# A two-layer kernel with a learned-weight 7x7 convolution: the position term of four of twelve slots is given as the bias of ScalarE's reads

## The chip, the cores and the metric

The kernel runs on one core of a Trainium2 chip. The metric is the device time of one execution in microseconds. Before the change the median of three runs is 3290.9 us (3275.71 to 3295.12). Everything is computed in float32.

## The reference, cut to what matters

The input has 4 images of 256 channels and 56 x 56 pixels. Layer 0 is the convolution in which the change lies; layer 1 is an attention with a squared score and a feed-forward part on selected tokens, and the change does not touch it.

```python
x1 = conv1x1(x, w1, b1)                       # 32 channels
x2 = conv1x1(x, w2, b2)                       # 32 channels
x3 = conv1x1(x, w3, b3)                       # 256 channels
p = conv1x1(position(h, w), wp, bp)           # 2 channels, the same for all images
sub2 = x1[:, :, None] - unfold_patches(x2)    # 49 shifts, reflected border
subp = p[:, :, None] - unfold_patches(p)
feat = concatenate([sub2, subp], axis=1)      # 34 channels, 49 shifts, 3136 pixels
y = relu(bn_eval(feat, bn1))
y = conv1x1(y, cw1)                           # 34 -> 32
y = relu(bn_eval(y, bn2))
wgt = softmax(conv1x1(y, cw2, cb2), axis=2)   # over the 49 shifts
out = sum over the 49 shifts of shifted(x3) * wgt, each weight shared by 8 channels
```

The "position term" is what the two channels of `subp`, after their normalisation and relu, add to the first hidden layer (`cw1`). `position` is linear along rows and along columns, so `p` minus shifted `p` is one constant for all pixels whose shifted pixel lies inside the image, and differs only where the border is reflected.

## The kernel before, in words

**Tiling.** The convolution works on blocks of 4 image rows: 14 blocks an image, 56 in all (`blocks`, line 417). A block has 4 x 56 = 224 pixels (`FB4`). The 48 shifts other than the centre are packed as 12 slots of 4 shifts each (`SLOTS`, line 79): a tile has 128 partitions, which are 4 shifts times 32 channels, and a slot is 224 columns of it. `PARTS` (line 86) splits the slots into part 0 (slots 0 to 7) and part 1 (slots 8 to 11, "the last four"). All of part 1 has the way `ROW`. The centre shift ("own") goes by its own small path.

**Steps of a block.** `relation` (line 521): `differ` subtracts on GpSimd into `y1`; `bend` is the relu of that on ScalarE, with nothing else; `hidden(i)` (line 558) makes the hidden layer of one part on TensorE into the PSUM tile `quad`, which has 4 banks, indexed by `r`, the row group of the matmuls; `bend_more(i)` (line 578) reads all four banks with relu, scale `s2` and bias `t2` into `y2`. `softmax` (line 600): `logits`, the maxima on VectorE, and later `lowered`, `exponents` and the sum. `values` (line 729): ScalarE copies a slot's weight to a PSUM bank (`weights`), VectorE multiplies it with the shifted values (`product`; GpSimd does slots 2, 5, 8 and 11), and TensorE adds the product into `acc` (`add`). `divide` makes `o`, and the result is stored.

**The hidden layer.** `hidden(i)` runs 16 matmuls of 32 x 32 (4 row groups by 4 column groups) and then 4 position matmuls, one for each row group, of 32 rows by 128 columns. With `m` = 2 for part 0 and 1 for part 1, these stream 448 or 224 columns of the constant tile `places` and accumulate into `quad`. `kind` (line 524) is 0 for the first block of an image, 2 for the last, 1 for the 12 between; it chooses the rows of weights in `cw1p`, so that one constant tile serves the three cases. `places` is made once, in `positions` (line 279), in the opening before the blocks.

**Order of the work.** Engines run in program order (`InOrder`, line 999; every instruction of the convolution so has line 1007 in the profile). The order is fixed by a table: each step of block k is entered at `k * ROUND + AT[name]`, with `ROUND` = 249 (line 109) and `AT` from line 110, and the entries are sorted. Near the change it is: `bend_1` 36, `bend_0` 51, `hidden_1` 52, `bend_more_1` 53, `values_1` 67, `hidden_0` 77, `bend_more_0` 90, `logits_0` 99, `largest_0` 126, `logits_1` 141. The adds and copies of the block before lie between these. There is one `quad`: `hidden_1`, `hidden_0`, `logits_0`, `logits_1`, `lowered_0` and `lowered_1` follow one another in it, and each waits until its last reader is done.

**Two kinds of round.** `planes` (line 295) prepares the normalised input in chunks of 8 image rows, one chunk in every second round until the input is used up. Such a round has more TensorE matmuls (`small<-xb` in the profile), two of them (`values_0` and `values_1`) on either side of `hidden_1`. The other rounds have `both` and `keep_both` of the same chunk, or no step of it at the end.

**Queues.** Nearly all transfers are issued by the SyncE queue; GpSimd issues indirect ones in layer 1.

Of the kernel before, what the change touches and what calls it, by code (L numbers as in the profile page):

```python
# [7 lines left out]
F32 = mybir.dt.float32  # L8
I32 = mybir.dt.int32
AF = mybir.ActivationFunctionType  # L10
ALU = mybir.AluOpType
# [4 lines left out]
P = 128  # L16
# [5 lines left out]
PAD = 3  # L22
# [31 lines left out]
def view(t, offset, dims):  # L54

    return bass.AP(t.tensor, t.offset + offset, [list(t.ap[0])] + [list(d) for d in dims])
# [29 lines left out]
PARTS = ((0, 8), (8, 12))  # L86
# [4 lines left out]
RB = 4  # L91
# [6 lines left out]
FB4 = RB * W  # L98
# [35 lines left out]
def conv_layer(  # L134
# [5 lines left out]
    const = ctx.enter_context(tc.tile_pool(name="conv_const", bufs=1))  # L140
# [5 lines left out]
    ve, te, se, sy, gp = (  # L146
        InOrder(tc, e) for e in (nc.vector, nc.tensor, nc.scalar, nc.sync, nc.gpsimd)
    )
# [3 lines left out]
    group = lambda g: slice(g * REL, (g + 1) * REL)  # L152
# [8 lines left out]
    def constant(name, of, shape):  # L161
        t = const.tile(shape, F32, name=name)
        nc.scalar.dma_start(t, of)
        return t
# [19 lines left out]
    cw1p = constant("cw1p", d["cw1_pos_tile"], [P, 3, P])  # L184
# [10 lines left out]
    quad = banks.tile([P, 4, 512], F32, name="quad")  # L195
# [10 lines left out]
    def bank():  # L206
        free.append(free.pop(0))
        return free[-1]
# [37 lines left out]

    tbc = const.tile([P, 1], F32, name="tbc")
    places = const.tile([P, 3 * FB4], F32, name="places")
    pp = opening.enter_context(tc.tile_pool(name="pos", bufs=1, side="right"))
    loc = pp.tile([P, 2, 2, 3 * FB4], F32, name="loc")  # L250
    nc.scalar.dma_start(loc, d["loc"])
# [27 lines left out]
    def positions():  # L279

        pl = pp.tile([P, 2, 3 * FB4], F32, name="pl")
        ve.tensor_scalar(pl, loc[:, 0], pposs[:, 4:5], None, ALU.mult)
        ve.scalar_tensor_tensor(pl, loc[:, 1], pposs[:, 5:6], pl, ALU.mult, ALU.add)
        ve.tensor_scalar(pl, pl, pposs[:, 6:7], None, ALU.add)
        ve.tensor_tensor(places, pl[:, 0], pl[:, 1], ALU.subtract)
        yield
        se.activation(places, places, AF.Relu, bias=tp1, scale=sp1)
        yield
        own = pp.tile([8, 1], F32, name="ownpos")
        se.activation(own, tp8, AF.Relu)  # L290
        p = bank()
        te.matmul(p[:, :1], cw1pd, own, start=True, stop=True)
        ve.tensor_scalar(tbc, p[:, :1], s2, t2, ALU.mult, ALU.add)
# [119 lines left out]
    y2 = [yp.tile([P, 4, (e - a) // 4, FB4], F32, name=f"y2_{a}") for a, e in PARTS]  # L413
# [107 lines left out]
    def relation(k):  # L521

        n, b = blocks[k]
        kind = 0 if b == 0 else 2 if b == last_block else 1

        def differ(i):
            aw, a1, _ = held["a", k]
            t = 3 * i
            ki, kj, way = SLOTS[t]
            if way == ROW:  # L530
                first, step = aw[:, ki : ki + RB, kj : kj + W], 1
            else:
                r = (4 * (COL_QUADS * n + b) + ki) % AC_KEPT
                first, step = ac[:, r : r + RB, kj : kj + W], WP
            gp.tensor_tensor(
                y1[:, t : t + 3].rearrange("p t (h w) -> p t h w", w=W),
                a1[:, :, PAD : PAD + W].unsqueeze(1).to_broadcast([P, 3, RB, W]),
                bass.AP(
                    first.tensor, first.offset,
                    [list(first.ap[0]), [step, 3], [WP, RB], [1, W]],  # L540
                ),
                ALU.subtract,
            )

        def differ_own():
            aw, _, aq = held["a", k]
            c = held["c1", k] = smp.tile([P, W], F32, tag="c1", name=f"c1_{k}")
            gp.tensor_tensor(c, aq, aw[:, PAD, PAD : PAD + W], ALU.subtract)

        def bend(i):  # L550
            a, e = PARTS[i]
            se.activation(y1[:, a:e], y1[:, a:e], AF.Relu)

        def bend_own():
            c = held["c1", k]
            se.activation(c, c, AF.Relu)

        def hidden(i):
            a, e = PARTS[i]
            m = (e - a) // 4  # L560
            for r in range(4):
                for j in range(4):
                    te.matmul(
                        quad[group(j), r, : m * FB4], cw1[group(r)],
                        view(y1[group(r)], (a + j) * FB4, [[4 * FB4, m], [1, FB4]]),
                        start=True, stop=False, skip_group_check=True,
                    )
            for r in range(4):
                te.matmul(
                    quad[:, r, : m * FB4], cw1p[group(r), kind],  # L570
                    places[group(r), a // 4 * FB4 : (a // 4 + m) * FB4],
                    start=False, stop=True, skip_group_check=True,
                )

        def hidden_own():
            quartered(small[:, :W], cw1d, held["c1", k], start=True, stop=True)

        def bend_more(i):
            m = (PARTS[i][1] - PARTS[i][0]) // 4
            se.activation(  # L580
                y2[i].rearrange("p r m f -> p r (m f)"), quad[:, :, : m * FB4], AF.Relu,
                bias=t2, scale=s2,
            )

        def bend_more_own():
            c = held["c2", k] = smp.tile([P, W], F32, tag="c2", name=f"c2_{k}")
            se.activation(c, small[:, :W], AF.Relu, bias=tbc, scale=s2)

        for i in range(4):
            yield f"differ_{i}", differ, (i,)  # L590
        yield "differ_own", differ_own, ()
        yield "bend_own", bend_own, ()
        yield "hidden_own", hidden_own, ()
        yield "bend_more_own", bend_more_own, ()
        for i in range(2):
            yield f"bend_{i}", bend, (i,)
            yield f"hidden_{i}", hidden, (i,)
            yield f"bend_more_{i}", bend_more, (i,)
# [281 lines left out]
    opening_steps = [{name: (do, of) for name, do, of in planes(0, q)} for q in range(3)]  # L880
    made_values = ("values_0", "keep_values_0", "values_1", "keep_values_1", "edges_values")
    placed = positions()
    for q in range(2):
        go(q, "normal_0", "normal_1", "both")
# [960 lines left out]
def tile_hybrid(tc: tile.TileContext, d, out: bass.AP):  # L1845
    with tc.tile_pool(name="scratch", bufs=1, space=DRAM) as dram:
        xs = dram.tile([NB, C, HW], F32, name="xs")
        us = [dram.tile([HW, ROW_N], F32, name=f"us{b}") for b in range(NB)]
        ln0 = dram.tile([C, HW], F32, name="ln0")
        rs0, rs0n = (dram.tile([1, HW], F32, name=f"rs0{i}") for i in "ab")  # L1850
        with tc.tile_pool(name="early", bufs=1) as pool:
            early = [
                pool.tile([P, *shape], F32, name=f"early{i}")
                for i, shape in enumerate(((2, 3 * C), (2, CH), (CH,)))
            ]
            conv_layer(tc, d, xs, ln0, rs0, rs0n, early)
            attn_ffn_layers(tc, d, xs, ln0, rs0n, us, out, early)
# [157 lines left out]
```

## Time and profile before

| | |
|---|---|
| median of three runs | 3290.9 us |
| lowest and highest run | 3275.71 and 3295.12 us |
| the profiled execution's own time | 3285.6 us |
| its span, first to last instruction | 3283.8 us |
| granted TensorE clock, mean over the span | 0.981 |
| position matmuls of 448 columns (part 0) | 448 instructions, 57.9 us busy |
| position matmuls of 224 columns (part 1) | 448 instructions, 38.8 us busy |
| ScalarE's read of `quad` for part 0, 128 x 1792 | 56 instructions, mean 1846 ns |
| ScalarE's read of `quad` for part 1, 128 x 896 | 56 instructions, mean 1091 ns |

How to read the lines of the profile: a group line gives the engine, the operation, the tile written and the tiles read (`quad<-places,cw1p`), the shape, the number of instructions, then the busy time in us and the mean of one in ns, and then how long the engine stood idle just before these and what ended it. A timeline line gives the start in us from the span's start, the length in us of a run of like instructions, and in square brackets the idle time before it with what released it. PE is TensorE's matmul, PEld its weight load, DVE VectorE, ACT ScalarE, POOL GpSimd, SP SyncE. A float32 matmul appears as two MATMUL instructions, so 4 position matmuls are 8 lines of the trace. Ends of matmuls are modelled, so a group's length reaches a little past the start of the next group.

### The profile page before, as it was taken

Reading aid. Unit: us, or ns where it says so; the run is one execution under the profiler, and the core shown is the slowest. Engines: PE = TensorE matmul, PEld = TensorE weight load, DVE = VectorE, ACT = ScalarE, POOL = GpSimd, SP = SyncE. Lnnn points to the kernel's source line nnn. Section 1 sums busy time; section 2 is a strip of 40 time slices with the busy share of each in tenths; the row PEclk is TensorE's granted clock in tenths of the full one; section 3 lists DMA queues with packets and bytes.
Section 4 is the critical chain, followed back from the end, with each engine's and each line's share of the span. In section 5 each row is a group of like instructions: output and inputs, shape, how many; then the busy total and the mean of one; then the engine's idle time right before and its main releaser. Section 6 shows DMA issues by size and latency. Waiting matters only on the chain. (4 is left out here: it accounts for less than half of the span.)

```text
span 3283.8 us, 108590 instructions
## 1 busy us (share of the span) xinstructions
PE 3040.2 (93%) x47392; PEld 1331.7 (41%) x47392; DVE 2230.9 (68%) x3022; ACT 1564.4 (48%) x2923; POOL 1722.4 (52%) x1223
## 2 busy tenths in 40 slices
PE   5999999999999999979999899989999899989899
PEld 2333333333333333324333443334333343356566
DVE  4888888998888888867455766567655765443121
ACT  4556566666566565523455244533455235531111
POOL 2899898999899899956101430236022430202311
PEclk8999999999999999989999999999999899999999
DMA  7656676567566655440122002310123001321110
GB/s 225 170 151 174 158 191 179 152 179 193 152 162 170 173 154 147 115 119 2 28 67 64 27 10 61 98 40 19 39 76 84 16 6 46 102 67 53 51 46 23
DMA packets 276930, 327.56 MB, mean 100 GB/s; under 512 B 96033, under 2 KB 270277, under 8 KB 276325
## 3 DMA queue, kind: packets, MB, share of 16 engines
q1 hardware_dynamic: 266469, 298.84, 34.5%
q0 software_dynamic: 7824, 19.48, 1.8%
q8 instruction: 372, 6.09, 0.8%
q10 hardware_dynamic: 2160, 2.29, 0.2%
q14 instruction: 105, 0.86, 0.1%
HBM read 251.51 MB, written 68.51 MB: 97 GB/s over the span
## 5 line engine op out<-in xcount | busy, mean ns | idle before, releaser
L1007 ACT ACTIVATE ph<-pg,unit 128x896 f32<-128x896 f32 x448 | 427.2, 1004 | 413.7 <-PE pg L1007 413.1
L1007 PE MATMUL acc<-pr,same 128*32 128x448 f32 x5376 | 595.8, 544 | 15.3 <-POOL pr L1007 8.3
L1007 POOL TENSOR_TENSOR phi<-ls 128x512 f32<-128x512 f32 (+1 forms) x200 | 247.0, 1235 | 494.8 <-issue 229.0
L1007 POOL TENSOR_TENSOR pr<-xw,w 128x1792 f32<-128x1792 f32 (+2 forms) x126 | 413.6, 3307 | 102.9 <-ACT exp L1007 80.0
L1007 DVE TENSOR_TENSOR pr<-xc,exp 128x1792 f32<-128x1792 f32 (+2 forms) x247 | 441.5, 1840 | 30.8 <-ACT exp L1007 27.5
L1007 DVE TENSOR_TENSOR pr<-xw,exp 128x1792 f32<-128x1792 f32 (+1 forms) x252 | 447.6, 1804 | 1.2 <-ACT exp L1007 1.2
L1007 POOL TENSOR_TENSOR pr<-xc,w 128x1792 f32<-128x1792 f32 (+1 forms) x135 | 419.6, 3117 | 9.6 <-ACT w L1007 6.6
L1007 POOL DMA_INDIRECT us<-rows,to x112 | 112.9, 1008 | 592.5 <-DVE rows L1007 329.3
L1007 DVE TENSOR_TENSOR phi<-pv,ls 128x1408 f32<-128x1408 f32 (+1 forms) x200 | 321.6, 1618 | 55.0 <-PE accs L1007 46.5
L1007 PE MATMUL quad<-y,cw 32*32 32x224 f32 (+1 forms) x10752 | 299.5, 456 | 30.6 <-ACT w L1007 18.8
L1007 PE MATMUL pg<-qT,pairs 32*128 32x448 f32 x1792 | 273.6, 587 | 6.2 <-ACT ph L1007 3.8
L1007 PE MATMUL pv<-early,xn 128*32 128x256 f32 x3136 | 220.9, 396 | 52.7 <-DVE phi L1007 34.1
L1007 ACT ACTIVATE ls<-pv 128x256 f32<-128x256 f32 (+1 forms) x200 | 77.4, 387 | 397.0 <-PE pv L1007 384.3
L1007 PE MATMUL accs<-phi,v 128*32 128x512 f32 (+1 forms) x1600 | 221.4, 617 | 32.0 <-DVE phi L1007 31.0
L1007 PEld LDWEIGHTS acc<-pr,same 128*32 128x32 f32 x5376 | 132.5, 109 | 240.2 <-issue 140.7
L1007 PE MATMUL acc<-ph,cf 128*32 128x448 f32 (+1 forms) x1792 | 215.5, 553 | 0.0
L1007 ACT ACTIVATE h<-ph,apar 128x512 f32<-128x512 f32 (+1 forms) x104 | 63.3, 659 | 295.6 <-PE ph L1007 295.6
L1007 DVE TENSOR_REDUCE mm<-quad 128x56 f32<-128x1792 f32 x112 | 172.7, 1542 | 32.2 <-PE quad L1007 32.1
L1007 ACT ACTIVATE y<-quad,bn2t,bn2s 128x896 f32<-128x896 f32 x112 | 164.5, 1468 | 63.0 <-PE quad L1007 63.0
L1007 POOL TENSOR_TENSOR y<-a,ac 128x672 f32<-128x672 f32 x112 | 171.0, 1526 | 36.3 <-DMA ac<-a12d 36.3
L1007 ACT ACTIVATE w<-quad,par 128x1792 f32<-128x1792 f32 x112 | 154.3, 1377 | 66.7 <-PE quad L1007 65.9
L1007 PEld LDWEIGHTS quad<-y,cw 32*32 32x32 f32 x10752 | 85.4, 103 | 244.0 <-issue 118.4
(282 smaller groups left out, 4960.2 us busy)
## 6 DMA issues: line engine op xcount, KB each, us to landing
xw<-x3d SPq DMA_DIRECT2D x54, 992.0 KB
xc<-x3d SPq DMA_DIRECT2D x58, 248.0 KB
xc<-x3d SPq DMA_DIRECT2D x58, 247.5 KB
xc<-x3d SPq DMA_DIRECT2D x58, 247.0 KB
xc<-x3d SPq DMA_DIRECT2D x58, 246.5 KB
x3d<-sx SPq DMA_DIRECT2D x28, 496.0 KB
xr<-in_x_own SPq DMA_DIRECT2D x56, 224.0 KB
xs<-xr SPq DMA_DIRECT2D x224, 56.0 KB
```

Source lines behind the costliest of these rows:

```text
L1007: return lambda *a, **k: self.tc.keep_in_program_order(of(*a, **k))
```

## The change

For part 1 the constant of the inner pixels is taken out of `places` and put into the bias of the second-layer read.

In the opening, `inner` takes one inner column of the last slot group of `places`, and that slot group has this column subtracted, so that its inner columns become zero. Twelve matmuls with one column each (4 row groups, 3 kinds) multiply `inner` by the position weights, and one VectorE instruction turns them into `lifts`, the bias of each kind and row group (times `s2`, plus `t2`).

In `hidden(1)`, in blocks of kind 1, the 4 position matmuls stream only the 3 left and 3 right columns of the 4 image rows, 24 columns in place of 224, in the pattern `[[W, 4], [W - PAD, 2], [1, PAD]]`. In blocks of kind 0 and 2 they keep 224 columns. Part 0 keeps its 448.

`bend_more(1)`, in all blocks, becomes four activations, one for each bank of `quad`, each with its own bias from `lifts`, 224 columns each, in place of one of 4 x 224. The step keeps its place in the order, and so does every other one.

```diff
@@ -246,6 +246,9 @@
     places = const.tile([P, 3 * FB4], F32, name="places")
+    LIFTED = PARTS[1][0] // 4
+    inner = const.tile([P, 1], F32, name="inner")
+    lifts = const.tile([P, 3, 4, 1], F32, name="lifts")
@@ -286,6 +289,20 @@
         se.activation(places, places, AF.Relu, bias=tp1, scale=sp1)
         yield
+        mine = places[:, LIFTED * FB4 : (LIFTED + 1) * FB4]
+        ve.tensor_copy(inner, mine[:, W // 2 : W // 2 + 1])
+        ve.tensor_tensor(mine, mine, inner.to_broadcast([P, FB4]), ALU.subtract)
+        yield
+        for r in range(4):
+            for kind in range(3):
+                te.matmul(
+                    quad[:, r, kind : kind + 1], cw1p[group(r), kind],
+                    inner[group(r)], start=True, stop=True,
+                )
+        ve.tensor_scalar(
+            lifts, view(quad, 0, [[1, 3], [512, 4], [1, 1]]), s2, t2, ALU.mult, ALU.add
+        )
+        yield
         own = pp.tile([8, 1], F32, name="ownpos")
@@ -565,10 +582,11 @@
+            of = [[W, m * RB], [W - PAD, 2], [1, PAD]] if i and kind == 1 else [[1, m * FB4]]
             for r in range(4):
                 te.matmul(
-                    quad[:, r, : m * FB4], cw1p[group(r), kind],
-                    places[group(r), a // 4 * FB4 : (a // 4 + m) * FB4],
+                    view(quad[:, r], 0, of), cw1p[group(r), kind],
+                    view(places[group(r)], a // 4 * FB4, of),
                     start=False, stop=True, skip_group_check=True,
                 )
@@ -577,6 +595,12 @@
         def bend_more(i):
             m = (PARTS[i][1] - PARTS[i][0]) // 4
+            for r in range(4 * i):
+                se.activation(
+                    y2[i][:, r, 0], quad[:, r, :FB4], AF.Relu, bias=lifts[:, kind, r], scale=s2
+                )
+            if i:
+                return
             se.activation(
                 y2[i].rearrange("p r m f -> p r (m f)"), quad[:, :, : m * FB4], AF.Relu,
                 bias=t2, scale=s2,
```

## The prediction, made before the changed kernel had run

> **What bounds the kernel now.** First the totals of the page, then the convolution alone (stretch table, 90 to 1430 us; columns are PE, PEld, DVE, ACT, POOL busy, granted clock, DMA share), since the change lies there only.
>
> ```profile
> PE 3040.2 (93%) x47392; PEld 1331.7 (41%) x47392; DVE 2230.9 (68%) x3022; ACT 1564.4 (48%) x2923; POOL 1722.4 (52%) x1223
> ```
>
> ```profile
> 90.00:1430.00 1340.00, 1283.83 (x26032) 495.75 (x26024) 1179.54 (x937) 811.78 (x1528) 1222.39 (x638) 1.00 0.61 161
> ```
>
> TensorE 96%, GpSimd 91%, VectorE 88%, ScalarE 61%: three engines near full, at full clock. None is "the" bound; the order of the hand-overs decides. So I read the timeline round by round. A round is one block of four image rows. Rounds 2, 4, ... 48 also prepare a chunk (matmuls `small<-xb`): 24 long rounds, about 24.4 us from one divide `o` to the next; 31 others are short, about 22.7 us; block 0 stands by itself. Short round, TensorE and then ScalarE:
>
> ```profile
> 814.47 0.67 PE L1007 MATMUL quad<-y,cw 32*32 32x224 f32 x32 [0.31 <-ACT w L1007]
> 815.08 0.66 PE L1007 MATMUL quad<-places,cw1p 32*128 32x224 f32 x8
> 815.67 0.96 PE L1007 MATMUL acc<-pr,same 128*32 128x448 f32 x8
> 816.80 0.96 PE L1007 MATMUL acc<-pr,same 128*32 128x448 f32 x8 [0.17 <-DVE pr L1007]
> 817.69 1.05 PE L1007 MATMUL quad<-y,cw 32*32 32x448 f32 x32
> 818.67 0.66 PE L1007 MATMUL quad<-places,cw1p 32*128 32x448 f32 x4
> ```
>
> ```profile
> 815.82 0.35 ACT L1007 ACTIVATE exp<-w 128x224 f32<-128x224 f32 x1
> 816.10 1.09 ACT L1007 ACTIVATE y<-quad,bn2t,bn2s 128x896 f32<-128x896 f32 x1
> 817.08 0.36 ACT L1007 ACTIVATE exp<-w 128x224 f32<-128x224 f32 x1
> 817.36 0.54 ACT L1007 ACTIVATE sa<-small,sh,bn1s 128x224 f32<-128x224 f32 x1
> 817.78 0.25 ACT L1007 ACTIVATE wo<-wo 128x56 f32<-128x56 f32 x1
> ```
>
> The fourth TensorE line is the one to see: the second add starts 1.13 us after the first, where adds one behind the other take 0.75 to 0.78, because VectorE's product ends at 816.7. What TensorE gains ahead of 816.8 is lost there. Long round:
>
> ```profile
> 838.17 0.68 PE L1007 MATMUL quad<-places,cw1p 32*128 32x224 f32 x8
> 838.77 1.77 PE L1007 MATMUL small<-xb,w 128*128 128x448 f32 x4
> 840.48 1.71 PE L1007 MATMUL acc<-pr,same 128*32 128x448 f32 x16
> 842.12 1.05 PE L1007 MATMUL quad<-y,cw 32*32 32x448 f32 x32
> 843.10 1.03 PE L1007 MATMUL quad<-places,cw1p 32*128 32x448 f32 x8
> ```
>
> Here nothing waits: TensorE is back to back. What it gains passes on to the add before GpSimd's third product (its buffer comes free there):
>
> ```profile
> 822.03 7.36 POOL L1007 TENSOR_TENSOR pr<-xw,w 128x1792 f32<-128x1792 f32 x2 [0.33 <-DMA ac<-a12d]
> ```
>
> ```profile
> 846.46 3.68 POOL L1007 TENSOR_TENSOR pr<-xw,w 128x1792 f32<-128x1792 f32 x1 [2.25 <-ACT exp L1007]
> ```
>
> In both kinds of round it starts 0.20 us after the modelled end of that add (821.83 and 846.26), whatever releaser the view names. TensorE, then two GpSimd products, then TensorE from 829.44 or 853.85: that is the chain, and time gained or lost by `hidden_0` is on it.
>
> **The change, part by part.**
>
> Position matmuls of the last four slots, 48 of the 56 blocks: 224 columns become 24. From group start to the next group 448 columns take 0.97 us and 224 take 0.59 (815.08 to 815.67), so 0.0017 us a column and, for 24, 0.25 us. The eight weight loads of this group alone span 0.31. Saved: 0.28 to 0.34, I take 0.30. No row shows a write in runs of three columns, so the other end is 0; the nearest row, `acc<-po` with 112 columns in two runs, takes 259 ns against 260 for a whole run (`small<-lsq`), so I stay at 0.30. The Trainium skill (PSUM — Partial Sum Buffer, Specifications (TRN2)) says that any non-contiguous pattern slows matmuls significantly. By the row the sum below stands; by that rule, taken as the saving lost, it would be 6.3 us higher, and no row here shows that.
>
> Second read of the hidden layer, all 56 blocks: one read of 896 becomes four of 224. The old one takes 1.09. The nearest row has the same shape, source and both pointers: `sa<-small`, 0.537 mean, and its follower starts 0.42 after it (817.36, 817.78). Four: 3 x 0.425 + 0.537 = 1.81, so +0.72 a block; bounds 1.68 (the `xr<-xr` pair's interval of 0.39) and 2.15 (no overlap). By the Trainium skill (ScalarE: Activation LUTs, What ACT_TABLE_LOAD costs) an activation costs 186 ns, 93 for each pointer, 0.833 per element, less 93 back to back: an estimate of +0.84, which would add 0.12 to each late round, some 4 us. ScalarE has 39% idle, so only two things matter.
>
> (a) Behind the reads on ScalarE stands the copy `exp<-w`, for which VectorE's next product waits. Short round: it lands at 817.44, becomes 818.16, and is needed at 818.65: free. Long round: it lands at 841.34, becomes 842.06, and is needed at 842.07: just free; what is late there has 0.83 us more cover, VectorE's later wait for `quad` at 847.65. ScalarE waits 0.46 and 0.70 us for others before its next read of `quad` and so catches up.
>
> (b) `hidden_0` overwrites `quad`. Behind it on TensorE's queue are its position term, the sums, the add that frees GpSimd's buffer, and the logits; ScalarE, GpSimd and VectorE wait for those. Each read now touches one bank, so I take it that each quarter of `hidden_0` waits for its own bank: free at 0.54, 0.96, 1.39 and 1.81 after the start. Short rounds: 816.10 + 1.81 + 0.05 (the hand-over from a `quad` reader at 825.25 to matmuls at 825.30) = 817.96; the last quarter starts now 0.12 behind the first, 817.81. Late by 0.15; in most short rounds `hidden_0` comes 0.07 earlier, so 0.22. I take 0.20; bounds 0.05 (reads of 1.68) and 0.34 (whole tile held). TensorE's 0.30 is not set against this: the product at 816.7 eats it, and the reads start behind ScalarE's own relu and copy, not behind TensorE. Long rounds: reads start 1.83 after the position term, last bank free at 3.69; the last quarter needs it at 3.95 - 0.30 + 0.12 = 3.77. Free, and all of the 0.30 passes. The three long edge rounds (no saving) lose nothing.
>
> Opening: a column copy, a subtraction, 24 one-column matmul passes, one small VectorE operation, once. They fall in TensorE's wait of 1.16 us before `small<-ownpos` (38.0 us) and VectorE's 12.5: nothing; about 1 us uncovered. Block 0's `hidden_0` has 0.27 us of room and gets 0.54 less: 0.4 with the smaller of these. No DMA is added, and none moves on SP's or GpSimd's queue.
>
> Sum: long interior rounds 21 x -0.30 = -6.3; short rounds 31 x +0.20 = +6.2; opening +0.4; together +0.3. The profiled execution took 3285.6 (span 3283.8 and 1.8 around it), 5.3 under the median shown, so 3285.9 here and 3291 beside that median.
>
> **The rivals.**
>
> *Whole-tile release.* `hidden_0` starts only when the fourth read ends: 31 x 0.34 = 10.5, long rounds gain 0.26 (3.95 to 3.69): -5.5. With 0.4: +5, 3296. For it: before, one read holds all four banks, so the trace cannot tell.
>
> *Reads wholly hidden.* Short rounds lose nothing and the DVE wait moves along with TensorE: 48 x 0.33 = -16, 3275. Against it: the add at 816.80.
>
> *No shorter matmul.* Runs of three cost as much as 224 columns: 0 - 0 + 6.2 + 0.4, 3298.
>
> *ScalarE becomes the bound (slower).* Place: the copy after the reads. If it reaches VectorE late in every round by the whole addition: 56 x 0.72 = +40, 3331. It decides once the copy is more than 0.5 us late in short rounds, that is, once the four reads take over 2.3 us. Against it: even without overlap they take 2.15. For it: long rounds have 0.01 us left before VectorE waits.
>
> **How the numbers follow.** Chances: forecast 0.45, whole-tile 0.24, hidden 0.14, no shorter 0.09, ScalarE bound 0.08. About 1% (33 us) is what a measurement of this kernel can tell from no change. Only the ScalarE case passes it upward: slower 0.08. Nothing worked out here passes it downward; 0.03 is left for a chain that I have misjudged. Within: 0.89. The low end is the hidden case less 5 us of the runs' own spread, 3270. The high end adds up the bad bounds: 31 x 0.34, no saving, and the copy exposed in the 24 long rounds (17.3): +28, 3319. Outside lie the ScalarE case and tails.
>
> **What would show it.** Right: a `quad<-places` group of 24 columns of about 0.3 us; four reads of about 0.54, 0.42 apart; short rounds about 0.2 longer, interior long rounds 0.3 shorter; the add at 816.80 still waiting for VectorE. Wrong: VectorE waiting for `exp` in short rounds; `hidden_0` starting at the last read (whole-tile); GpSimd's third product no later in short rounds.

## The result and the profile after

The changed kernel takes 3296.43 us (median of 20 runs, 3288.43 to 3318.36) against 3286.37 for the kernel before in the same comparison (20 runs, 3275.71 to 3295.12). The ratio is 1.0036 with a 95% interval of 1.0023 to 1.0049: about 12 us slower (7.6 to 16), where the forecast was +0.3. That is still inside the 1% that the forecast called no change and inside its range, but the interval, of 0.13% to either side, excludes zero, so a term of the sum was off. The forecast came out right because its range also held the case of a rival, and that rival is what happened: the case it chose, a release bank by bank, did not. The profiled execution of the changed kernel has a time of 3294.97 and a span of 3293.2 us.

First the totals and the stretch of the convolution from the profile after (columns as before: PE, PEld, DVE, ACT, POOL busy, granted clock, DMA share).

```profile
PE 3026.9 (92%) x47416; PEld 1331.3 (40%) x47416; DVE 2237.6 (68%) x3025; ACT 1602.3 (49%) x3091; POOL 1721.9 (52%) x1223
```

```profile
90.00:1430.00 1340.00, 1263.32 (x25882) 492.71 (x25872) 1170.42 (x926) 844.49 (x1679) 1205.88 (x634) 1.00 0.62 161
```

TensorE has 13 us less work in all, ScalarE 38 us more, and the time grew: no total of busy time tells the outcome. In the fixed stretch GpSimd fell from 1222 to 1206 us because the stretch now holds less of the work (634 of its instructions instead of 638). The cause has to be read in the rounds. The same short round as in the prediction, TensorE and then ScalarE, after the change:

```profile
823.71 0.42 PE L1031 MATMUL quad<-places,cw1p 32*128 32x24 f32 x8
824.06 0.96 PE L1031 MATMUL acc<-pr,same 128*32 128x448 f32 x8
825.43 0.96 PE L1031 MATMUL acc<-pr,same 128*32 128x448 f32 x8 [0.41 <-DVE pr L1031]
826.69 1.05 PE L1031 MATMUL quad<-y,cw 32*32 32x448 f32 x32 [0.30 <-ACT y L1031]
827.66 1.03 PE L1031 MATMUL quad<-places,cw1p 32*128 32x448 f32 x8
```

```profile
824.45 0.35 ACT L1031 ACTIVATE exp<-w 128x224 f32<-128x224 f32 x1
824.73 1.81 ACT L1031 ACTIVATE y<-quad,lifts,bn2s 128x224 f32<-128x224 f32 x4
826.42 0.37 ACT L1031 ACTIVATE exp<-w 128x224 f32<-128x224 f32 x1
```

Three things are to be seen. The position group, 823.71 to the next group at 824.06, is 0.35 us instead of 0.59. The second add now waits 0.41 for VectorE where it waited 0.17: what TensorE gained is lost there, as forecast. And the fourth line has a wait that was not there: `hidden_0` (`quad<-y`, 448 columns) waits 0.30 for ScalarE. The four reads end at 824.73 + 1.81 = 826.54, and `hidden_0` starts at 826.69, 0.15 behind the end of the last of them (0.144 before rounding). It was not released bank by bank. Measured from the start of the position group it starts at 2.98 us instead of 2.54 (the medians; 2.61 in the round shown before). GpSimd's third product follows:

```profile
831.02 7.35 POOL L1031 TENSOR_TENSOR pr<-xw,w 128x1792 f32<-128x1792 f32 x2 [0.69 <-ACT exp L1031]
```

It starts 7.31 us after the position group, which is also the median of the short rounds; before, the median was 6.88. The lateness of `hidden_0`, 0.44, arrives there almost whole (0.43).

The long round behind it, TensorE and ScalarE:

```profile
847.16 0.43 PE L1031 MATMUL quad<-places,cw1p 32*128 32x24 f32 x8
847.52 1.77 PE L1031 MATMUL small<-xb,w 128*128 128x448 f32 x4
849.23 1.71 PE L1031 MATMUL acc<-pr,same 128*32 128x448 f32 x16
850.95 1.05 PE L1031 MATMUL quad<-y,cw 32*32 32x448 f32 x32
```

```profile
848.99 1.81 ACT L1031 ACTIVATE y<-quad,lifts,bn2s 128x224 f32<-128x224 f32 x4
```

`hidden_0` starts at 850.95, that is at 3.79 instead of 3.95. The reads end at 850.80, 0.15 ahead of it again: TensorE could have come 0.25 earlier and is held for the last 0.09, although the view shows no wait there.

The median starts of `hidden_0`, in us after the position group of part 1, over all rounds of one profile, and the median change of a round's length. A round's length is taken from one position group of part 1 to the next and compared with the same round of the profile before; of the long rounds, the 21 interior ones count:

| kernel | short rounds | long rounds | round's length, short / long | time against before |
|---|---|---|---|---|
| before | 2.54 | 3.95 | |  |
| after | 2.98 | 3.79 | +0.45 / -0.14 | +11.8 us |
| `e1_narrow_only` | 2.54 | 3.70 | +0.01 / -0.26 | 0.0 |
| `e9_narrow_no_opening` | 2.54 | 3.71 | +0.02 / -0.24 | -8.5 |
| `e2_four_reads_only` | 2.97 | 3.95 | +0.41 / +0.01 | +14.5 |
| `e10_four_reads_long_rounds` | 2.54 | 3.95 | 0.00 / +0.03 | -0.3 |
| `e6_read_behind_copy` | 3.15 | 3.95 | +0.61 / +0.02 | +12.5 |
| `e7_eight_reads_only` | 3.95 | 4.76 | +1.40 / +0.81 | +66 |

The last column is the ratio less one, times 3286 or so; the intervals stand with each experiment. A ratio is worked out from all timed runs of a comparison, so it can differ a little from the quotient of the two medians. Single profiles differ by several us through rounds that wait for transfers, so the last column is from the timed rounds and not from spans.

### The profile page after: what moved, and what is told of

Its sections match the earlier page's. It is cut to its first block, busy times and chain, and to the rows that moved or that the text cites. A ratio compares the mean times of both kernels' runs of the same rounds, so it can differ in the third digit from the quotient of the medians.

```text
span 3293.2 us, 108812 instructions
## 1 busy us (share of the span) xinstructions
PE 3026.9 (92%) x47416; PEld 1331.3 (40%) x47416; DVE 2237.6 (68%) x3025; ACT 1602.3 (49%) x3091; POOL 1721.9 (52%) x1223
## 5 line engine op out<-in xcount | busy, mean ns | idle before, releaser
L1031 ACT ACTIVATE exp<-w 128x224 f32<-128x224 f32 x448 | 156.9, 355 | 45.2 <-DVE pr L1031 43.5
```

The source lines that it names most:

```text
L1031: return lambda *a, **k: self.tc.keep_in_program_order(of(*a, **k))
```

## The experiments

Three theories were set against one another. **Release**: the loss comes from `hidden_0`, which waits for the end of the last read, in the short rounds, and the gain comes from the long interior rounds alone. **Whole saving**: the shorter matmuls gain in all 48 interior blocks, some 12 us, and the reads cost still more, some 22. **Load**: the added ScalarE time itself is what costs, by making ScalarE's copies late for VectorE.

### The matmuls alone, and the reads alone

`e1_narrow_only` is the changed kernel with the one read and one bias of before:

```diff
-            for r in range(4 * i):
-                se.activation(
-                    y2[i][:, r, 0], quad[:, r, :FB4], AF.Relu, bias=lifts[:, kind, r], scale=s2
-                )
-            if i:
-                return
```

> The changed kernel with one read of the second part, with bias t2, in place of four: the matmuls of 24 columns alone. It leaves the constant of the inner pixels out of the result. The changed kernel is about 10 us over the one before. Theory Release (TensorE's gain counts only in the long rounds; the loss is hidden_0 waiting for the last of the four reads in short rounds): the position group takes 0.35 in place of 0.60, hidden_0 comes 0.25 earlier in the 21 long interior rounds and not at all in short ones, so about -5 us, ratio 0.998 to 0.999. Theory Whole saving (the gain counts in all 48 interior blocks and the reads cost some 22 us): 48 x 0.25 = -12 us, ratio 0.996. Theory Load (the loss is ScalarE's added time, which makes its copies late for VectorE): the gain is as in one of the two, no loss.

Measured: 3285.87 against 3283.69, ratio 1.0000 (0.9983 to 1.0016). A saving of 12 us is outside this interval, unless the opening's work gives it back (see `e8_opening_only`). The 5 us that Release expected from the long rounds lie just inside it: they are neither seen nor excluded, although `hidden_0` does start at 3.70 there.

`e2_four_reads_only` is the kernel before with four reads, all with the bias `t2`:

```diff
+            for r in range(4 * i):
+                se.activation(
+                    y2[i][:, r, 0], quad[:, r, :FB4], AF.Relu, bias=t2, scale=s2
+                )
+            if i:
+                return
```

> The kernel before with four reads of one bank each, all with bias t2; the position matmuls keep 224 columns; the result is the same. Theory Release: short rounds lose 0.43 (hidden_0 from 2.54 to 2.98 us after the position term), long ones nothing (the last read ends at 3.64, hidden_0 stands at 3.95): 31 x 0.43 + 0.5 = +14 us, ratio 1.004. Theory Whole saving: +22 us, ratio 1.007. Theory Load: 56 x 0.72 at the most, between +14 and +40 us, with VectorE waiting for copies longer than before in long rounds also.

Measured: 3300.79 against 3283.69, ratio 1.0044 (1.0027 to 1.0062), +14.5 us. The four reads alone cost all of the loss and a little more.

`e3_two_reads_only` reads two banks at a time:

```diff
+            for r in range(0, 4 * i, 2):
+                se.activation(
+                    y2[i][:, r : r + 2, 0], quad[:, r : r + 2, :FB4], AF.Relu, bias=t2, scale=s2
+                )
+            if i:
+                return
```

> The kernel before with two reads of two banks each, bias t2, the result the same: ScalarE's time per block grows by about 0.22 in place of 0.72. Theory Release: the last read ends at 1.02 + 1.31 = 2.33 after the position term, with 0.15 of hand-over at 2.48, before the 2.54 at which hidden_0 stands in most short rounds: 0 to +2 us, ratio 1.000 to 1.0006. Theories Whole saving and Load: a share of 0.22 / 0.72 of what four reads cost, +4 to +7 us, ratio 1.0013 to 1.002.

Measured: 3288.71 against 3283.69, ratio 1.0006 (0.9990 to 1.0022). No cost can be told from zero. In the short round the two reads end just early enough for `hidden_0`:

```profile
823.97 1.33 ACT L1013 ACTIVATE y<-quad,bn2t,bn2s 128x448 f32<-128x448 f32 x2
```

The position group of this round is at 822.95 in its profile, so the reads end at 2.35; `hidden_0` keeps its median of 2.54. ScalarE's added time is a third of that of four reads (0.24 against 0.72), so this run alone does not part Release from Load.

### The change only where it should pay

`e4_long_rounds_only` narrows the matmuls and splits the reads in the 21 long interior rounds alone; the others have the kernel's old form. `places` stays whole, and a small tile `border` holds the subtracted border columns.

```diff
+        lifted = kind == 1 and k % 2 == 0 and k <= 48
...
+            of = [[W, m * RB], [W - PAD, 2], [1, PAD]] if i and lifted else [[1, m * FB4]]
...
+                    border[group(r)] if i and lifted
+                    else view(places[group(r)], a // 4 * FB4, of),
...
+            for r in range(4 * i * lifted):
```

> The change made only in the 21 interior blocks whose round is long; the other 35 keep the whole constant tile and one read. The result is the same as before. Theory Release: hidden_0 stands at 3.79 in place of 3.95 us in these rounds and where it was in short ones: 21 x -0.16 = -3 us, ratio 0.999, perhaps not to be told from 1. Theory Load (late copies cost as much as four reads, in proportion to the rounds): 21 / 56 of ScalarE's part of the loss less the gain of 21 x 0.25, 0 to +3 us.

Measured: 3283.44 against 3285.92, ratio 0.9994 (0.9977 to 1.0012). No loss and no gain can be told from zero; the typical long interior round is 0.14 shorter, which would make 21 x 0.14 = 3 us. This is the version that the readings point to, and it is not shown to beat the kernel before.

### ScalarE's time without a hold, and a hold without ScalarE's time

`e5_scalar_load` adds three small activations behind the read of before. They write tiles that nothing reads and touch no part of `quad`:

```diff
+            for t in spare if i else ():
+                se.activation(t, places[:, :8], AF.Relu, bias=t2, scale=s2)
```

> The kernel before with its one read, and behind it three ScalarE instructions of 8 columns each into tiles that nobody reads: about 0.73 us more on ScalarE at the same place, as the four reads add, but quad is released when it was before. The result is the same. Theory Release: 0 to +2 us, ratio 1.000 to 1.0006, and hidden_0 at 2.54 and 3.95 us as before. Theory Load: the same loss as four reads alone, +14 us or more, ratio 1.004 or more, with VectorE waiting for copies.

Measured: 3289.26 against 3283.69, ratio 1.0021 (1.0007 to 1.0034), +7 us (2 to 11). That is more than Release expected, and the Load theory has a part in it. The three take 0.95 us, more than the 0.72 that the change adds. Where they hurt is to be read in round 29 of that profile, VectorE and then ScalarE:

```profile
769.58 4.00 DVE L1010 TENSOR_TENSOR pr<-xc,exp 128x1792 f32<-128x1792 f32 x2
774.17 2.02 DVE L1010 TENSOR_TENSOR pr<-xc,exp 128x1792 f32<-128x1792 f32 x1 [0.59 <-ACT exp L1010]
```

```profile
772.95 0.95 ACT L1010 ACTIVATE spare<-places,bn2t,bn2s 128x8 f32<-128x8 f32 x3
773.79 0.34 ACT L1010 ACTIVATE exp<-w 128x224 f32<-128x224 f32 x1
...
774.86 1.03 ACT L1010 ACTIVATE lsq<-lt 128x448 f32<-128x448 f32 x2
```

The same three products run without a gap in the kernel before:

```profile
766.49 5.93 DVE L1007 TENSOR_TENSOR pr<-xc,exp 128x1792 f32<-128x1792 f32 x3
```

Here VectorE waits 0.59 for a copy (`exp`) that ScalarE makes only after the added work. The two squares for the next layer's norm (`lsq`) belong to the same round but come behind that copy, so they do not delay it. What differs is how early VectorE wants it: in the kernel before, the copy of round 29 was ready 0.20 us before VectorE's next product started, and in the round that the prediction read, 1.15. The wait occurs in short rounds 1, 9, 13, 19, 29, 33, 39 and 45, with 0.36 to 1.30 us each and 5.9 together, and in none of them in the kernel before (waits over 0.15 us count); that is most of the 7 us.

`e6_read_behind_copy` is the opposite test. The read stays one, with no work added, but is entered behind a copy of the block before, so that it ends later:

```diff
-    "keep_values_0": 47, "bend_0": 51, "hidden_1": 52, "bend_more_1": 53, "values_1": 67,
+    "keep_values_0": 47, "bend_0": 51, "hidden_1": 52, "bend_more_1": 71, "values_1": 67,
```

> The kernel before with its one read of the second part moved behind the next copy of a weight (its place in the order 71 in place of 53); nothing is added to ScalarE, and that copy comes earlier for VectorE. The result is the same. Theory Release: in short rounds the copy waits until VectorE frees its bank, 1.64 us after the position term; the read then runs from 1.9 to 3.0, hidden_0 at 3.1 in place of 2.54: 31 x 0.59 = +18 us, ratio 1.0055; long rounds are as before. Theory Load: 0 or a little less, ratio 0.999 to 1.000.

Measured: 3298.89 against 3285.92, ratio 1.0038 (1.0019 to 1.0058), +12.5 us. A late release alone, with ScalarE's work as before, costs as much as the whole change. The short round shows it, ScalarE and TensorE:

```profile
832.31 1.08 ACT L1007 ACTIVATE y<-quad,bn2t,bn2s 128x896 f32<-128x896 f32 x1
```

```profile
831.98 0.96 PE L1007 MATMUL acc<-pr,same 128*32 128x448 f32 x8 [0.17 <-DVE pr L1007]
833.54 1.20 PE L1007 MATMUL quad<-y,cw 32*32 32x448 f32 x32 [0.60 <-ACT y L1007]
```

The read ends at 833.39 and `hidden_0` starts 0.15 later. Over the 30 short rounds that have a next round, without the latest one, `hidden_0` starts 0.49 later on average than before (2.95 against 2.46): 31 x 0.49 = 15, of which 12.5 was measured (6 to 19 by the interval).

`e7_eight_reads_only` doubles the suspected hold: eight reads of half a bank, bias `t2`.

```diff
+            for r in range(4 * i):
+                for f in (slice(0, FB4 // 2), slice(FB4 // 2, FB4)):
+                    se.activation(
+                        y2[i][:, r, 0, f], quad[:, r, f], AF.Relu, bias=t2, scale=s2
+                    )
+            if i:
+                return
```

> The kernel before with eight reads of half a bank each, bias t2, the result the same; ScalarE gets some 1.65 us more a block. Theory Release: the reads last 7 x 0.33 + 0.43 = 2.74; short rounds: hidden_0 at 1.02 + 2.74 + 0.15 = 3.91 in place of 2.54, 31 x 1.37 = +42; long rounds: 4.72 in place of 3.95, 24 x 0.77 = +18; together +61 us, ratio 1.0185. Theory Load, in proportion to what ScalarE's time alone cost (7 us for 0.73): +16 us, ratio 1.005; in proportion to four reads (14.5 us for 0.72): +33 us, ratio 1.010.

Measured: 3354.56 against 3285.92, ratio 1.0200 (1.0173 to 1.0226), +66 us. Release, with the hold now in the long rounds as well, had 1.0185. The short round:

```profile
857.18 2.79 ACT L1014 ACTIVATE y<-quad,bn2t,bn2s 128x112 f32<-128x112 f32 x8
```

```profile
857.88 0.96 PE L1014 MATMUL acc<-pr,same 128*32 128x448 f32 x8 [0.17 <-DVE pr L1014]
860.12 1.21 PE L1014 MATMUL quad<-y,cw 32*32 32x448 f32 x32 [1.27 <-ACT y L1014]
```

The reads end at 859.97, and once more `hidden_0` starts 0.15 behind the last. In the long rounds, where four reads were free, it now waits 0.74 and starts at 4.76. VectorE also waits for the copy behind the reads here, in 29 of the 30 short rounds that have a next round, so not all of the 66 us has to be the hold.

### The opening, and the matmuls without it

`e8_opening_only` adds the opening's work to the kernel before, with the subtraction into a tile that nothing reads:

```diff
+        ve.tensor_copy(inner, mine[:, W // 2 : W // 2 + 1])
+        ve.tensor_tensor(pl0, mine, inner.to_broadcast([P, FB4]), ALU.subtract)
...
+                te.matmul(
+                    quad[:, r, kind : kind + 1], cw1p[group(r), kind],
+                    inner[group(r)], start=True, stop=True,
+                )
```

> The kernel before with the opening of the change alone: the column, the subtraction (into a tile that nobody reads), the 24 one-column passes and the bias are made and not used. The result is the same. Both theories: 0 to +1 us, ratio 1.000. If it is +4 us or more, part of the loss is the opening's.

Measured: 3291.02 against 3285.92, ratio 1.0014 (0.9995 to 1.0032): not to be told from zero. The prediction gave the new instructions nothing, or about 1 us if nothing covers them.

`e9_narrow_no_opening` has the 24-column pattern of `hidden(1)` alone:

```diff
+            of = [[W, m * RB], [W - PAD, 2], [1, PAD]] if i and kind == 1 else [[1, m * FB4]]
```

> The kernel before with the 24-column position matmuls alone: no opening work, the constant tile is left whole, one read of 896 columns with the one bias. It leaves out the position term of the inner pixels of the last four slots in the interior blocks. The narrow matmuls with the opening measured 1.000 (0.998 to 1.002), the opening alone 1.0014. Release: the position group shortens from 0.59 to 0.35 us; short rounds keep hidden_0 at 2.54 us, since the read starts behind ScalarE's copy; long interior rounds have hidden_0 at about 3.70 instead of 3.95 and gain: 21 x 0.25 = 5 us, ratio 0.9985 (0.997 to 1.000). If the long rounds' gain is lost again further on (at GpSimd or VectorE), the ratio is 1.000 although hidden_0 starts at 3.70. Whole saving: 48 x 0.25 = 12 us, ratio 0.9963.

Measured: 3277.74 against 3285.78, ratio 0.9974 (0.9961 to 0.9987), -8.5 us (-13 to -4). So the shorter matmuls do gain. Four lines of its profile tell where; a short round, then a long one:

```profile
815.07 0.42 PE L1008 MATMUL quad<-places,cw1p 32*128 32x24 f32 x8
816.78 0.96 PE L1008 MATMUL acc<-pr,same 128*32 128x448 f32 x8 [0.41 <-DVE pr L1008]
...
838.15 0.43 PE L1008 MATMUL quad<-places,cw1p 32*128 32x24 f32 x8
841.86 1.05 PE L1008 MATMUL quad<-y,cw 32*32 32x448 f32 x32
```

In the short round the add waits for VectorE 0.24 longer, and `hidden_0` stays at 2.54; in the long one it starts at 3.71, 0.24 earlier. In 4 short rounds, where VectorE is early enough, it starts at 2.00 instead of 2.25. 25 x 0.25 = 6 us is worked out from these; the interval holds that and also the 12 of the Whole saving (just), so the time of this run does not part the two, nor does that of `e1_narrow_only` if its opening costs over 6 us, which `e8_opening_only` leaves possible. The rounds part them: in both profiles the median short round has `hidden_0` at 2.54 as before and keeps its length (+0.01 and +0.02), so no saving passes there.

`e10_four_reads_long_rounds` puts four reads with the bias `t2` into the 24 long rounds alone:

```diff
+            long = i == 1 and 0 < k <= 48 and k % 2 == 0
+            for r in range(4 * long):
+                se.activation(
+                    y2[i][:, r, 0], quad[:, r, :FB4], AF.Relu, bias=t2, scale=s2
+                )
```

> The kernel before with four reads of one bank each (the same bias t2) in the 24 long rounds alone; the other rounds keep the one read and nothing else is changed. Release: in long rounds the last read ends 1.83 + 1.81 = 3.64 us after the position group starts, TensorE comes to hidden_0 at 3.95 anyway, so nothing is late: ratio 1.000 (0.999 to 1.001). Load: the added 0.72 us of ScalarE in 24 of 56 rounds costs its share of what ScalarE work of 0.95 us without any hold of quad cost in all rounds (7 us): 24/56 x 7 = 3 us, ratio 1.001; at its share of what the four reads cost in all rounds (14.5 us), 6 us, ratio 1.002.

Measured: 3286.98 against 3285.78, ratio 0.9999 (0.9984 to 1.0013). The long round, ScalarE and TensorE:

```profile
847.08 1.82 ACT L1014 ACTIVATE y<-quad,bn2t,bn2s 128x224 f32<-128x224 f32 x4
```

```profile
845.26 0.68 PE L1014 MATMUL quad<-places,cw1p 32*128 32x224 f32 x8
849.21 1.05 PE L1014 MATMUL quad<-y,cw 32*32 32x448 f32 x32
```

The reads end at 848.90; TensorE comes at 849.21 anyway. Reads with the same ScalarE time each cost 14.5 us when they stand in all rounds, and here nothing that can be told from zero. This excludes the 6 us of Load at its share of the four reads' cost, and not its 3 us.

The pieces add up: the matmuls -8.5, the opening +4.6 (with an interval from -1.6), the four reads +14.5, together +10.6; the whole change measured +11.8. With intervals of 4 to 6 us to either side of each piece, this is agreement and no proof.

## Why the prediction was off by 12 us

**What bounds the kernel** was right. No engine's total decides; TensorE's way into GpSimd's third product does. Where `hidden_0` was late, that product was late by the same (0.43 of 0.44), and so was the whole short round (0.45).

**The position matmuls** were right in kind; the saving was taken a little too large: the group went from 0.59 to 0.35, so 0.24 was saved, where 0.30 was taken out of 0.28 to 0.34. The rule cited there, that a non-contiguous pattern slows matmuls significantly (the Trainium skill, PSUM — Partial Sum Buffer, Specifications (TRN2)), would have left the saving at nothing; the row of 24 columns in runs of three says otherwise. Whether the pattern costs something smaller this case does not show: the 0.35 lies above both the 0.25 worked out by columns and the 0.31 of the weight loads.

```profile
L1031 PE MATMUL quad<-places,cw1p 32*128 32x24 f32 x384 | 20.5, 275 | 0.0
L1031 PE MATMUL quad<-places,cw1p 32*128 32x224 f32 x64 | 5.8, 431 | 0.0
```

**The four reads** were right to the hundredth: 1.81 us, +0.72. The estimate worked out from the Trainium skill (ScalarE: Activation LUTs, What ACT_TABLE_LOAD costs) was +0.84; the measurement decides for the row. (The lower bound given, 1.68, should be 3 x 0.39 + 0.537 = 1.71; only the lower bound of the lateness, 0.05, rests on it.)

**(b), "each quarter of `hidden_0` waits for its own bank", is the step that failed.** `hidden_0` was released as a whole, 0.15 us after the end of the last read, in the changed kernel and in the experiments with one read (`e6`) and with eight (`e7`) alike. An engine tells another that an instruction is done by raising a counter, a semaphore, which the waiting instruction watches. In the trace of the changed kernel, of each block's four reads only the last raises ScalarE's semaphore (56 of 224 reads), and the first matmul of `hidden_0` waits for that.

The size of the hand-over was wrong with it. It was taken as 0.05, from a matmul that waits for VectorE; here it is 0.14 to 0.15. The difference does not go with the engine that signals but with the number of semaphores waited for: `hidden_0` waits for two, ScalarE's and GpSimd's. In the profile after, matmuls that wait for one semaphore, with TensorE idle for over 0.15 us before them, started 0.05 to 0.06 behind the end of the instruction that the profile names as their releaser, whether that was on ScalarE (42 of 43), VectorE (85 of 85) or GpSimd (44 of 44); with two or more it was 0.14 to 0.15 (ScalarE 56 of 60, VectorE 37 of 42). No run changed that number alone, so why it is so stays open. The profile before showed it already: this read of `quad` ends at 814.33, and `hidden_1`, the first TensorE line of the short round in the prediction, starts at 814.47.

```profile
813.32 1.01 ACT L1007 ACTIVATE w<-quad,par 128x896 f32<-128x896 f32 x1 [0.31 <-PE quad L1007]
```

And so the lateness is 0.44 in a typical short round (0.45 on average) instead of 0.20, outside the bounds given (0.05 to 0.34): 31 x 0.45 = 14 us instead of 6.2. `e2_four_reads_only` measures 14.5 for it.

**"All of the 0.30 passes" in long rounds** failed by the same step: the release at 3.79 cuts the gain to 0.16, 21 x 0.16 = 3.4 us instead of 6.3. With the hand-over of 0.05 the release would have come at 3.69 and cost nothing there. Without the four reads (`e9`) the long rounds have the whole 0.24.

**(a), the copy behind the reads, "free" in short rounds,** held in the round that was read and not in all. In the rounds where VectorE wants it early, it comes late. Round 29 in the changed kernel, then in `e2_four_reads_only`:

```profile
779.30 2.02 DVE L1031 TENSOR_TENSOR pr<-xc,exp 128x1792 f32<-128x1792 f32 x1 [0.23 <-ACT exp L1031]
...
780.24 2.02 DVE L1013 TENSOR_TENSOR pr<-xc,exp 128x1792 f32<-128x1792 f32 x1 [0.48 <-ACT exp L1013]
```

In the changed kernel these waits stand in short rounds 9, 13, 19, 29 and 39, 1.2 us together; in `e2` in 9, 19, 29 and 39, 1.9 us together; in the profile before in none. (In rounds 1, 7, 11 and 23 of `e2` VectorE waits 0.70 to 0.94 for the copy ahead of the reads, which they cannot delay; before, it waits 0.51 for such a copy in round 39.) So, as far as VectorE's waits for the copy behind the reads tell, Load is a small part: some 1 of the 11.8 us and some 2 of the 14.5. And they do not simply add to the hold: rounds 19, 29 and 39 of `e2` are 0.43 to 0.44 longer than before, where the median short round is 0.41 longer. In long rounds, "just free" was right (`e10`).

**"The product at 816.7 eats it"** was right: the add's wait for VectorE grew from 0.17 to 0.41, and `e9` shows the same without the reads. The rival of reads wholly hidden falls there.

**The opening** went into the sum with 0.4, for block 0's `hidden_0`; the prediction's own figures give 0.54 - 0.27 = 0.27. It starts 3.17 us after its position group instead of 2.52, so 0.65 later (one profile each; in the other profiles with one read it is 2.39 to 2.82). The new instructions were costed at nothing, and in TensorE's queue that is nearly so. After the change:

```profile
34.85 3.17 PE L1031 MATMUL exp<-x,w 128*128 128x448 f32 x8
37.95 1.46 PE L1031 MATMUL quad<-inner,cw1p 32*128 32x1 f32 x23
...
40.02 1.06 PE L1031 MATMUL quad<-x,w 128*64 128x224 f32 x8 [0.47 <-ACT x L1031]
```

From the first of these lines to the last it is 5.17 us, and 4.98 before (33.68 to 38.66): 0.2 us. Yet `e8` measured +4.6 (-1.6 to +10.5), and `e1` and `e9`, which differ by the opening and its tiles alone, lie 8.5 us apart, with intervals that just overlap. Whether something of the opening costs some us stays open: the typical round of `e8` is as long as before (+0.01 and +0.02). The sum does not need it: 14 for the short rounds, -3.4 for the long ones and 0.65 for block 0 make about +11, and +11.8 was measured.

**The rivals.** *Whole-tile release* was the one that happened, with its sum too small: 3296 was right beside the median of 3290.9 that was shown, but as a difference it said +5 and +11.8 was measured, since the hand-over was 0.15 and the saving 0.24. *Reads wholly hidden* took 0.33 a round where the sum had 0.30. *No shorter matmul* is excluded by the group of 24 columns. *ScalarE becomes the bound* needed the copy late in every round; in the changed kernel it is late in five of the 31 short ones, by 0.22 to 0.24, and four reads in the long ones cost nothing that shows (`e10`).

## What to carry to other kernels

Here splitting one read of a buffer into several smaller ones made the buffer free only when the last of them ended, because only that one signalled. Unless the program shows a separate signal for each, cost such a split as (number of reads x interval) against the slack of the next writer, stage by stage. The slack differs between rounds that look alike: here four reads were free in 24 rounds and cost 14 us in the other 31, and the copy behind them was late in a few of those. So measure slack in every kind of round, by the median of all its rounds, and look for the rounds that are off it. Look up in the program which instruction sends the signal before assuming a finer release than the trace shows, and take a hand-over time from an instruction that waits for as many semaphores.

## What the runs showed of the hardware

- Small activations are dear by their number: 896 columns took 1.09 us in one, 1.33 in two, 1.81 in four and 2.79 in eight. Each further instruction was 0.24 us, at 448, 224 and 112 columns alike.
- A hand-over to an idle TensorE took 0.05 to 0.06 us where the matmul waits for one semaphore and mostly 0.14 to 0.15 where it waits for two or more, from ScalarE and VectorE alike (the counts stand above).
- Position matmuls of 24 columns come at 0.35 us for the group of eight instructions, of 224 at 0.59 and of 448 at 0.96 (the prediction read 0.97): from 224 columns down to 24 saves 0.24 and not in proportion.
